# A four-layer decoder on one core: the LSTM's gates turned in two pieces, the third batch's attention moved beside the second batch's picks, and gathers tied to the blocks beside them

## The chip, the cores and the metric

The kernel runs on one core of one Trainium2 chip. The metric is the device time of one execution in microseconds (us); lower is better. The core has a matrix engine (PE), a vector engine (DVE), an activation engine (ACT), a general engine (POOL) and a queue engine (SP), each with an instruction stream of its own that it works off in order. They meet only at semaphores. SP and POOL issue the DMA transfers; POOL alone issues those whose rows are looked up in an index (gathers and scatters).

## The reference, cut to what matters

A batch of 4 sequences of 512 tokens of 256 numbers, `x`, goes through four layers. Each adds a gated attention and then a gated feed-forward block to `x`:

```
x = x + tanh(g_xattn[0]) * L0_xattn(ctx, layernorm(x))   # LSTM that attends to 64 context rows
x = x + tanh(g_ffn[0])   * L0_ffn(layernorm(x))          # 8 experts, the best one
x = x + tanh(g_xattn[1]) * L1_xattn(layernorm(x), ctx)   # attention both ways
x = x + tanh(g_ffn[1])   * L1_ffn(layernorm(x))          # 8 experts, the best two
x = x + tanh(g_xattn[2]) * L2_xattn(layernorm(x), ctx)   # additive attention
x = x + tanh(g_ffn[2])   * L2_ffn(layernorm(x))          # 8 experts, as many as make up 0.8
x = x + tanh(g_xattn[3]) * L3_xattn(layernorm(x), ctx)   # 16 heads
x = x + tanh(g_ffn[3])   * L3_ffn(layernorm(x))          # 8-bit product
```

The three pieces that the change touches:

```
# L0_xattn, one of 512 steps in order
e = tanh(f_proj + (h0 @ Wh)[:, None, :]); alpha = softmax(e . v); attn = alpha @ feats
i, f, g, o = split(x @ W_ih.T + h @ W_hh.T + b)          # four gates of 256
c = sigmoid(f) * c + sigmoid(i) * tanh(g); h = sigmoid(o) * tanh(c)

# L2_xattn: for each token, 64 context rows, 256 features
rho = sum_d w_d * tanh(txt_proj + feat_proj + b); att = softmax(rho); ...

# L2_ffn: probs sorted, kept while their running sum stays under 0.8 (the first always)
y = sum over kept experts of prob * (relu(x @ W1[e] + b1[e]) @ W2[e] + b2[e])
```

## The kernel before, in words

**The LSTM** (`recurrence`, `lstm_step`) takes the first 3444 us. One step turns the state of step t into that of t + 1: PE multiplies `h` (into `psa` and `psf`), DVE turns `psa` into `hw` and adds it to the context's projection (`e`), ACT takes the tanh, PE sums it over the features (`psr`), DVE and ACT make the softmax (`stat`, `al`, `alb`), PE adds the attention's part to the gates in `psf` [128, 256], and then comes the piece that is changed: DVE turns `psf` into `gt` in 32 x 32 blocks (line 958), PE starts the next step's input part in `psf` (`gates_of_x`, line 557), ACT takes one tanh of all four gates (line 961, 32 numbers in each partition), DVE makes `u` and the new cell state from i, f and g (965, 969), ACT its tanh `tcn` (971), DVE the new `h` from gate o and `tcn` (976). The order of these instructions is written out by hand (`pin`). The first layer's experts fill the gaps: a planner (`Later`) hands PE, ACT, DVE, POOL and SP a few of their instructions at fixed places of a step.

**The other three layers** are the tail, 3444 to 5437 us. Here the order is written as generators that yield after each small piece. `weave(main, side, ratio)` emits `ratio` pieces of `side` after each piece of `main`; `chain` and `turns` put generators one after the other and in turns. PE's order is the order of emission (`Ordered`); DVE, ACT, POOL and SP are ordered by the framework's scheduler from priorities and readiness, and each then works in order. A branch closes a basic block, and the scheduler orders within one.

The main lines are the blocks of experts. Tokens of two batches form a group. `picks_of` (by `sorted_by`) ranks the experts of a batch's tokens and scatters each token's row to its experts' places in DRAM (`rows`, line 1306: 8 scatters of 128 rows for each batch in layer 1, 24 in layer 2). `Blocks` then runs over 128 (layer 1) or 256 rows (layer 2) of one expert: `load` fetches rows and weights (SP), `turn` transposes the rows (PE into PSUM, DVE to `xT`, line 1437), `work_1` and `work_2` multiply, `out` copies 128 result rows out of PSUM (`y`) and stores them to `res`. 20 blocks of a group are always emitted (`sure`); `rest` runs any further ones under a branch. A block of layer 2 is 7 pieces (four of the up product, a turn, two of the down product). `b0`, `b1` are layer 1's two groups, `c0`, `c1` layer 2's. `back` gathers the results for each token from `res` (line 1560: 16 gathers for each group in layer 1, 48 in layer 2) into six buffers `yg`, and DVE adds them to `xtok` (line 1552).

The sides are the attentions of the next layer: `additive` (`l2(b)`, 77 pieces; its core is 128 tanh on ACT and their products on PE into `psr`), `heads` and `quantised` for layer 3, and the picks. In the order before, the side of `b1` is: gathers of group 0, attention of batch 0, attention of batch 1 in turns with the picks of batch 0, picks of batch 1. The side of `c0` is the same for batches 2 and 3. The side of `c1` begins with the 48 gathers of layer 2's group 0.

The pieces of the order that the change touches:

Of the kernel before, what the change touches and what calls it, by code (L numbers as in the profile page):

```python
# [24 lines left out]
AF = mybir.ActivationFunctionType  # L25
# [5 lines left out]
NB, S, D = 4, 512, 256  # L31
# [521 lines left out]
def gates_of_x(net, out, ge, t):  # L553

    sel = net.ident.rearrange("p (b t) -> p b t", b=NB)[:, :, t % 32]
    for q in range(4):
        net.tc.keep_in_program_order(net.nc.tensor.matmul(  # L557
            out[32 * q : 32 * q + NB, :], lhsT=sel, rhs=ge[t // 32][:, ts(q, 256)],
            start=True, stop=False,
        ))  # L560
# [330 lines left out]
def lstm_step(net, sp, ps, w, later, ge, t, h, hnew, cnew, ga, ganext):  # L891
    nc = net.nc
    pin = net.tc.keep_in_program_order
    psf = ps["f"]
# [60 lines left out]
    later.fill("PE", SLOT_C)  # L955

    gt = sp.tile([P, 8, 32], FP, name="gt")
    pin(nc.vector.transpose(gt.rearrange("p g b -> p (g b)"), psf))  # L958
    if t + 1 < S:
        gates_of_x(net, psf, ge, t + 1)  # L960
    pin(nc.scalar.activation(  # L961
        ga[:, 0:4].rearrange("p g c b -> p (g c) b"), gt[:, :, 0:NB], AF.Tanh, scale=0.5
    ))
    u = sp.tile([P, 2, 2, NB], FP, name="u")
    pin(nc.vector.scalar_tensor_tensor(
        u.rearrange("p g c b -> p g (c b)"), ga[:, 0:2].rearrange("p g c b -> p g (c b)"), 1.0,
# [22 lines left out]
def weave(main, side, ratio):  # L989

    due = 0.0
    for _ in main:
        due += ratio
        while due >= 1:
            due -= 1
            next(side, None)
    for _ in side:
        pass


def run(pieces):
    for _ in pieces:
        pass


def chain(*gens):
    for g in gens:
        yield from g
# [84 lines left out]
def load_router(net, layer, pool):  # L1093
    nc, a = net.nc, net.a
    m = {"wr": pool.tile([P, KD, NE], FP, name=f"wr{layer}")}
    nc.sync.dma_start(m["wr"], a[f"L{layer}_wr"])
    if layer == 2:
        for n, shape in (("br", [P, NE]), ("b2", [NE, D])):
            m[n] = pool.tile(shape, FP, name=f"m2_{n}")
            src = a[f"L2_{n}"]  # L1100
            nc.sync.dma_start(m[n], src.partition_broadcast(P) if n == "br" else src)
    return m
# [249 lines left out]
class Blocks:  # L1352
# [87 lines left out]
    def out(self, i, half, ps):  # L1440
        y = self.pool.tile([P, D], FP, name=f"y_{self.kind.layer}", bufs=3)
        if i >= self.on_scalar:
            self.t.nc.scalar.copy(y, ps)
        else:
            self.t.nc.vector.tensor_copy(y, ps)
        self.dma(self.got["res"][ds(self.row(i) + half * P, P), :], y)

    def some(self, lo, hi, at=None):
# [95 lines left out]
def back(t, pool, kind, batches, group, got):  # L1544


    net, nc = t.net, t.nc
    due = deque()

    def add():  # L1550
        for y, xj, c in due.popleft():
            nc.vector.scalar_tensor_tensor(xj, y, c, xj, ALU.mult, ALU.add)  # L1552

    for b in batches:
        for i in range(TPB):
            for k in range(0, kind.most, 2):
                here = []
                for kk in (k, k + 1):
                    y = pool.tile([P, D], FP, name="yg", bufs=6)
                    nc.gpsimd.indirect_dma_start(  # L1560
                        out=y[:, :], out_offset=None, in_=got["res"][:, :],
                        in_offset=bass.IndirectOffsetOnAxis(
                            ap=got["index"][:, b - group[0], kk, i : i + 1], axis=0
                        ),
                    )
                    c = got["cw"][:, b - group[0], kk, i : i + 1]
                    here.append((y, net.xtok[:, b * TPB + i, :], c))
                due.append(here)
                if len(due) > 2:
                    add()  # L1570
                yield
    while due:
        add()
        yield
# [23 lines left out]
def gate_bias(t, w, pool):  # L1598

    w["hbg"] = pool.tile([P, 2], FP, name="hbg")  # L1600
    t.nc.vector.tensor_scalar_mul(w["hbg"], w["b"][:, 6, :], 0.5)
# [412 lines left out]
def turns(*gens):  # L2014

    gens = list(gens)
    while gens:
        for g in list(gens):
            try:
                next(g)  # L2020
            except StopIteration:
                gens.remove(g)
            yield


def part_of(gen, n):

    for _ in range(n):
        if next(gen, gen) is gen:
            return  # L2030
        yield
# [3 lines left out]
def gated_blocks_kernel(ctx: ExitStack, tc: tile.TileContext, a, out):  # L2035
    net = Net(ctx, tc, a)
# [18 lines left out]
    }  # L2055
    lstm(net)
    t = Tail(net, ctx)
    t.last = None, None
    mp = ctx.enter_context(tc.tile_pool(name="routers", bufs=1))
    t.rows = mp.tile([P, 3, GB, D], FP, name="rows_in")  # L2060
    t.b1 = mp.tile([P, 3, F_MOE[2] // P], FP, name="b1_in")
    with right, ExitStack() as work:

        def beside(name, bufs):
            return right.enter_context(tc.tile_pool(name=name, bufs=bufs, side="right"))

        p2 = beside("attn2", 1)
        sort, first = beside("sort", 1), beside("first", 2)
        pool = {"sort": sort, "got": mp}
        m = {1: load_router(net, 1, mp), 2: load_router(net, 2, mp)}  # L2070
        with tc.tile_pool(name="attn1", bufs=1) as p1:
            w1 = load_l1(net, p1)
            w2 = load_l2(net, p2)
            gate_bias(t, w1, p1)
            pk = Picks(t, sort)

            def l1(b):
                return both_ways(t, w1, p1, b)

            def l2(b):  # L2080
                return additive(t, w2, p2w, b)

            def behind(layer, part, b):

                return chain(
                    part(b), turns(sorted_by(layer, b), part(b + 1)), sorted_by(layer, b + 1)
                )

            def sorted_by(layer, b):
                g, n = divmod(b, GB)  # L2090
                return picks_of(t, pk, pool, KINDS[layer], m[layer], b, n, got[layer][g])

            b1 = Blocks(t, KINDS[1], first, got[1][1], KINDS[1].sure % 3)
            b0 = Blocks(t, KINDS[1], first, got[1][0], 0, b1)
            run(behind(1, l1, 0))
            weave(b0.sure(), chain(behind(1, l1, 2), constants_l2(t, w2, p2)), 1.1)
            b0.rest()
        one = ctx.enter_context(tc.tile_pool(name="second", bufs=2))
        p2w = work.enter_context(tc.tile_pool(name="attn2_work", bufs=1))
        c1 = Blocks(t, KINDS[2], one, got[2][1], (2 * KINDS[1].sure + KINDS[2].sure) % 3, on_scalar=0)  # L2100
        c0 = b1.next = Blocks(t, KINDS[2], one, got[2][0], 2 * KINDS[1].sure % 3, c1, on_scalar=12)

        def back_of(layer, g, batches=None):
            return back(t, one, KINDS[layer], batches or groups[g], groups[g], got[layer][g])

        weave(b1.sure(), chain(back_of(1, 0), behind(2, l2, 0)), 2.7)
        b1.rest()
        weave(c0.sure(), chain(back_of(1, 1), behind(2, l2, 2)), 2.0)
        c0.rest()
    p3 = ctx.enter_context(tc.tile_pool(name="attn3", bufs=1))  # L2110
    w3 = load_l3(net, p3)
# [125 lines left out]
```

## Time and profile before

Three timed runs took 5443.04, 5443.75 and 5444.30 us (median 5443.75). The profiled execution took 5438.9 us, of which its span from the first instruction to the last is 5437.2.

| | |
|---|---|
| LSTM, 54 to 3444 us | 512 steps, 6.62 us each |
| tail, 3444 to 5437 us | 1993 us |
| busy PE, DVE, ACT, POOL of the span | 4618.9, 2444.1, 2531.7, 467.7 us |
| granted PE clock, mean | 0.959 |
| blocks `b1` with attention of batches 0 and 1 | from 3944 us |
| first row of POOL's 24 scatters of batch 1, layer 2 | 4266.82 us |
| first up product of `c0` | 4309 us |
| first piece of `c1` | 4761 us |
| layer 3 alone | from 5145 us |

A line of the timeline gives start, duration, engine, source line, operation, `out<-in`, shapes and count; in brackets stands how long the engine idled before it and what ended that. A line of the stage windows gives the busy time (and number of records) of PE, PE's weight loads, DVE, ACT and, where it worked, POOL, the granted PE clock as a share of full speed, and DMA. A product in 32-bit numbers leaves two PE records.

### The profile page before, as it was taken

How to read it: one execution, taken by the hardware profiler on the slowest of the kernel's cores; microseconds unless marked ns; L12 is line 12 of the kernel's file. 1: busy time of each engine (PE TensorE's matmuls, PEld its weight loads, DVE VectorE, ACT ScalarE, POOL GpSimd, SP SyncE). 2: the span in 40 equal slices, each digit the busy share in tenths (PEclk: the TensorE clock that was granted, in tenths of full speed). 3: DMA queues.
4: the chain of work that ended last, by engine and by line, in shares of the span. 5: the costliest groups of instructions: out<-in, count | busy, mean ns of one | idle time of the engine just before them, and what ended most of it. 6: DMA issues, size and time to landing. Idle time of an engine off the chain costs nothing. (4 is left out here: it accounts for less than half of the span.)

```text
span 5437.2 us, 139292 instructions
## 1 busy us (share of the span) xinstructions
PE 4618.9 (85%) x57536; PEld 2505.2 (46%) x57536; DVE 2444.1 (45%) x9788; ACT 2531.7 (47%) x7114; POOL 467.7 (9%) x884
## 2 busy tenths in 40 slices
PE   6756698889999899999999989987988599879967
PEld 3222244334444344444444434764533365767734
DVE  4555555555555555555555555224422332222245
ACT  2233465456656566565566556421276166223212
POOL 1000000100100100000000000001111201130030
PEclk9999999999999999999999999988998699889978
DMA  5000012122222122122122211313543333454210
GB/s 196 18 2 2 10 72 109 42 79 97 87 76 95 54 91 95 62 76 95 72 81 79 87 43 56 107 52 126 198 143 128 131 117 129 166 178 142 84 53 8
DMA packets 117964, 480.48 MB, mean 88 GB/s; under 512 B 23473, under 2 KB 62786, under 8 KB 87938
## 3 DMA queue, kind: packets, MB, share of 16 engines
q1 hardware_dynamic: 105026, 437.85, 22.5%
q0 software_dynamic: 12288, 33.57, 1.8%
q8 instruction: 456, 7.47, 0.6%
q14 instruction: 194, 1.59, 0.1%
HBM read 434.65 MB, written 137.89 MB: 105 GB/s over the span
## 5 line engine op out<-in xcount | busy, mean ns | idle before, releaser
L950 PE MATMUL psf<-fw,alb 128*4 128x256 f32 x8192 | 538.7, 380 | 142.4 <-DVE alb L946 111.1
L803 PE MATMUL ps_up<-xm,ring 128*128 128x256 f32 x2048 | 614.8, 412 | 3.4 <-ACT h L813 3.3
L834 PE MATMUL ps_down<-ring,h 128*128 128x256 f32 x2048 | 581.0, 400 | 0.0
L908 PE MATMUL psf<-whh,hb 128*4 128x256 f32 x8176 | 538.0, 381 | 0.0
L803 PEld LDWEIGHTS ps_up<-xm,ring 128*128 128x128 f32 x2048 | 335.9, 188 | 226.7 <-issue 174.1
L938 ACT ACTIVATE al<-psr,stat 128x64 f32<-128x64 f32 x1024 | 313.2, 310 | 272.0 <-DVE stat L937 271.4
L917 ACT ACTIVATE e<-e 128x256 f32<-128x256 f32 x512 | 213.5, 417 | 465.1 <-DVE e L916 464.1
L834 PEld LDWEIGHTS ps_down<-ring,h 128*128 128x128 f32 x2048 | 357.1, 189 | 157.4 <-issue 112.2
L937 DVE TENSOR_REDUCE stat<-psr 128x1 f32<-128x64 f32 x1024 | 229.5, 225 | 417.3 <-PE psr L926 407.7
L916 DVE TENSOR_TENSOR e<-fproj,hw 128x256 f32<-128x256 f32 x1024 | 395.4, 427 | 17.6
L899 PE MATMUL psa<-wh,hb 128*4 128x64 f32 x8176 | 208.3, 219 | 229.4 <-DVE hb L976 228.3
L926 PE MATMUL psr<-e,vrep 128*32 128x64 f32 x16384 | 347.2, 223 | 38.5 <-ACT e L917 33.0
L977 POOL COPY cb<-ga 128x8 f32<-128x8 f32 x512 | 97.9, 191 | 3214.0 <-DVE ga L969 3214.0
L1778 ACT ACTIVATE h<-featT,cx_txtT 128x512 f32<-128x512 f32 x512 | 324.0, 710 | 99.4 <-PE psr L1019 61.2
L557 PE MATMUL psf<-ge,ident 128*4 128x256 f32 x4096 | 318.0, 382 | 60.3 <-DVE gt L958 60.2
L926 PEld LDWEIGHTS psr<-e,vrep 128*32 128x32 f32 x16384 | 260.1, 109 | 223.8 <-ACT e L917 216.4
L958 DVE STREAM_TRANSPOSE gt<-psf 128x256 f32<-128x256 f32 x512 | 230.5, 450 | 292.6 <-PE psf L950 292.2
L961 ACT ACTIVATE ga<-gt 128x32 f32<-128x32 f32 x512 | 116.9, 228 | 525.3 <-DVE gt L958 525.1
L1019 PE MATMUL ps_up<-xT,ring 128*128 128x256 f32 x1280 | 313.2, 396 | 53.6 <-ACT h L1508 26.8
L950 PEld LDWEIGHTS psf<-fw,alb 128*4 128x4 f32 x8192 | 117.1, 84 | 495.0 <-DVE alb L946 493.8
L899 PEld LDWEIGHTS psa<-wh,hb 128*4 128x4 f32 x8176 | 113.7, 85 | 486.8 <-DVE hb L976 486.8
L1019 PEld LDWEIGHTS ps_up<-xT,ring 128*128 128x128 f32 x1280 | 245.8, 197 | 132.9 <-issue 48.2
(410 smaller groups left out, 6595.2 us busy)
## 6 DMA issues: line engine op xcount, KB each, us to landing
ring<-in_L_w_dram SPq DMA_DIRECT2D x208, 1024.0 KB
ring<-in_L_w_dram SPq DMA_DIRECT2D x120, 512.0 KB
res<-y SPq DMA_DIRECT2D x120, 128.0 KB
rows_in<-rows SPq DMA_DIRECT2D x40, 256.0 KB
rows_in<-rows SPq DMA_DIRECT2D x40, 128.0 KB
rows<-in_x_dram SPq DMA_DIRECT2D x2, 1920.0 KB
res<-in_x_dram SPq DMA_DIRECT2D x2, 1920.0 KB
xtok<-in_x_dram SPq DMA_DIRECT2D x4, 512.0 KB
```

The costliest lines, as they stand in the source:

```text
L557: net.tc.keep_in_program_order(net.nc.tensor.matmul(out[32 * q : 32 * q + NB, :], lhsT=sel, rhs=ge[t // 32][:, ts(q, 256)], start=True, st ...
L803: yield nc.tensor.matmul(cell["ps"][:, f % 2, :], lhsT=ex["w"][:, k, ts(f, P)], rhs=box["x"][:, k, :], start=k == 0, stop=k == KD - 1,)
L834: yield nc.tensor.matmul(cell["ps"], lhsT=ex["h"][:, f, ts(p, P)], rhs=ex["down"][:, f, :], start=f == 0, stop=f == 7,)
L899: pin(nc.tensor.matmul(ps["a"][32 * q : 32 * q + NB, :], lhsT=h[:, c, :], rhs=w["wh"][:, c, ts(q, 64)], start=c == 0, stop=c == 1,))
L908: pin(nc.tensor.matmul(psf[32 * q : 32 * q + NB, :], lhsT=h[:, c, :], rhs=w["whh"][:, c, ts(q, 256)], start=False, stop=False,))
L916: pin(nc.vector.tensor_add(e[:, p], w["fproj"][:, p], bc(hw[:, :, ts(p, 2)], 3, SC)))
L926: pin(nc.tensor.matmul(ps["r"][p][ts(2 * b + i, 32), :], lhsT=w["vrep"][:, c, :], rhs=ev[:, ::-1, :] if i else ev, start=c == 0, stop=c == ...
L938: pin(nc.scalar.activation(al[:, p], ps["r"][p], AF.Exp, bias=stat[:, p, 0:1], accum_out=stat[:, p, 1:2]))
L950: pin(nc.tensor.matmul(psf[32 * q : 32 * q + NB, :], lhsT=alb[:, p], rhs=w["fw"][:, p, ts(q, 256)], start=False, stop=p == 1,))
L958: pin(nc.vector.transpose(gt.rearrange("p g b -> p (g b)"), psf))
L1019: return lambda *a, **k: self.tc.keep_in_program_order(fn(*a, **k))
L1778: nc.scalar.activation(h, featT[:, ec, :], AF.Tanh, bias=w["txtT"][:, ec, col : col + 1])
```

## The change

1. `lstm_step`: the turn of `psf` and the tanh are made in two pieces, columns 0 to 192 (gates i, f, g) and 192 to 256 (gate o): turn, tanh, turn, tanh. `gates_of_x` is emitted after both.
2. `out` keeps the instruction that copies a block's result and its basic block in `t.mark`. In `back`, a gather of layer 2 (`kind.most > 2`) gets a semaphore wait on the latest such copy that has been emitted in the same basic block.
3. The picks of batch 1 leave the side of `b1` (ratio 2.3 for 2.7). They run after `b1` and before `c0`, in turns with the first 42 pieces of batch 2's chain (its 8 gathers and their adds, then its attention). The rest of that chain, batch 3's gathers, its attention in turns with the picks of batch 2, and the picks of batch 3 are the side of `c0` (ratio 1.6 for 2.0).

```diff
@@ lstm_step
-    pin(nc.vector.transpose(gt.rearrange("p g b -> p (g b)"), psf))
+    for lo, hi in ((0, 6), (6, 8)):
+        pin(nc.vector.transpose(
+            gt[:, lo:hi].rearrange("p g b -> p (g b)"), psf[:, 32 * lo : 32 * hi]
+        ))
+        pin(nc.scalar.activation(
+            ga.rearrange("p g c b -> p (g c) b")[:, lo:hi], gt[:, lo:hi, 0:NB], AF.Tanh, scale=0.5
+        ))
     if t + 1 < S:
         gates_of_x(net, psf, ge, t + 1)
-    pin(nc.scalar.activation(
-        ga[:, 0:4].rearrange("p g c b -> p (g c) b"), gt[:, :, 0:NB], AF.Tanh, scale=0.5
-    ))
@@ Blocks.out
-            self.t.nc.scalar.copy(y, ps)
+            x = self.t.nc.scalar.copy(y, ps)
...
-            self.t.nc.vector.tensor_copy(y, ps)
+            x = self.t.nc.vector.tensor_copy(y, ps)
+        self.t.mark = x.ins, self.t.net.nc.cur_bb
@@ back
-                    nc.gpsimd.indirect_dma_start(
+                    x = nc.gpsimd.indirect_dma_start(
...
+                    if kind.most > 2 and t.mark[1] is net.nc.cur_bb:
+                        net.tc.add_manual_dep(
+                            x.ins, t.mark[0].name, mybir.DependencyInfo(
+                                mybir.DependencyClass.Sync, mybir.DependencyReason.DATA
+                            ), reason="in step with the blocks beside it",
+                        )
@@ gated_blocks_kernel
-        weave(b1.sure(), chain(back_of(1, 0), behind(2, l2, 0)), 2.7)
+        weave(b1.sure(), chain(back_of(1, 0), l2(0), turns(sorted_by(2, 0), l2(1))), 2.3)
         b1.rest()
-        weave(c0.sure(), chain(back_of(1, 1), behind(2, l2, 2)), 2.0)
+
+        ahead = chain(back_of(1, 1, [2]), l2(2))
+        run(turns(sorted_by(2, 1), part_of(ahead, 42)))
+        weave(
+            c0.sure(), chain(
+                ahead, back_of(1, 1, [3]), turns(sorted_by(2, 2), l2(3)), sorted_by(2, 3)
+            ), 1.6,
+        )
         c0.rest()
```

`part_of(gen, n)` yields the first n pieces of a generator and leaves the rest in it; `behind(layer, part, b)` is `chain(part(b), turns(sorted_by(layer, b), part(b + 1)), sorted_by(layer, b + 1))`.

More of the change, by code (lines that the diff above doesn't have):

```diff
@@ L2057, in gated_blocks_kernel @@
     t = Tail(net, ctx)
-    t.last = None, None
+    t.last = t.mark = None, None
     mp = ctx.enter_context(tc.tile_pool(name="routers", bufs=1))
```

## The prediction

> **What bounds the kernel now.** I read the stage windows first, then the timeline of one LSTM step and the list of who waits for `gt`, then the timeline around the two changed places of the tail. The windows (columns: PE, PE's weight loads, DVE, ACT, POOL, PE clock, DMA):
>
> ```profile
> 54.00:3444.00 3390.00, 2922.02 (x49827) 1379.42 (x49824) 1791.69 (x7971) 1822.99 (x5838) 191.01 (x593) 1.00 0.18 66
> ...
> 3966.00:4222.00 256.00, 227.08 (x943) 88.80 (x941) 73.15 (x216) 189.63 (x314) 23.96 (x25) 0.94 0.37 126
> 4222.00:4271.00 49.00, 35.21 (x117) 23.81 (x116) 26.52 (x116) 9.97 (x15) 3.27 (x4) 0.69 0.12 40
> 4271.00:4309.00 38.00, 1.24 (x5) 0.87 (x5) 4.09 (x11) 0.00 (x0) 28.91 (x30) 0.52 0.55 195
> 4309.00:4328.00 19.00, 10.80 (x38) 8.51 (x38) 10.18 (x29) 0.30 (x1) 6.70 (x7) 0.68 0.49 159
> 4328.00:4776.00 448.00, 414.43 (x2024) 286.37 (x2023) 124.86 (x394) 216.25 (x374) 56.57 (x58) 0.94 0.42 145
> 4776.00:4831.00 55.00, 18.28 (x64) 14.85 (x65) 22.63 (x55) 6.06 (x13) 35.72 (x37) 0.66 0.46 145
> 4831.00:5145.00 314.00, 308.86 (x1513) 248.34 (x1514) 55.09 (x108) 95.03 (x212) 2.08 (x2) 1.00 0.39 135
> ```
>
> In the LSTM no engine is full: a chain through all of them sets each step. In the tail PE is the bound (448 and 314 us at 93% and 98%) but for two holes: from 4271 to 4328 us, while POOL scatters the picks of batch 1, and from 4776 to 4831, while POOL gathers. The chain of a step:
>
> ```profile
> 2001.71 0.45 DVE L958 STREAM_TRANSPOSE gt<-psf 128x256 f32<-128x256 f32 x1 [0.35 <-PE psf L950]
> 2002.26 0.23 ACT L961 ACTIVATE ga<-gt 128x32 f32<-128x32 f32 x1 [1.97 <-DVE gt L958]
> 2002.52 0.18 DVE L965 SCALAR_TENSOR_TENSOR u<-ga 128x16 f32<-128x16 f32 x1 [0.36 <-ACT ga L961]
> ...
> 2002.81 0.17 DVE L969 SCALAR_TENSOR_TENSOR ga<-u 128x8 f32<-128x8 f32 x1
> ...
> 2003.07 0.21 ACT L971 ACTIVATE tcn<-ga 128x8 f32<-128x8 f32 x1 [0.58 <-DVE ga L969]
> ...
> 2003.54 0.41 PE L899 MATMUL psa<-wh,hb 128*4 128x64 f32 x16 [0.28 <-DVE hb L976]
> ```
>
> Each starts when the one above ends. Of the 512 steps, ACT waited for `gt` in these, says the list for that tile; in the other 217 it was still at work on the first layer's gelu:
>
> ```profile
>   DVE gt L958: 525.1, 295
> ```
>
> The second hole, at the start of `c1`:
>
> ```profile
> 4776.12 0.37 ACT L1443 COPY y<-ps_down 128x256 f32<-128x256 f32 x1 [6.74 <-PE ps_down L1019]
> ...
> 4783.26 0.68 DVE L1437 COPY xT<-ps_side 128x512 f32<-128x512 f32 x1
> ...
> 4784.00 7.53 PE L1019 MATMUL ps_up<-xT,ring 128*128 128x256 f32 x24 [8.15 <-DVE xtok L1552]
> ...
> 4811.25 0.37 ACT L1443 COPY y<-ps_down 128x256 f32<-128x256 f32 x1 [34.76 <-remote]
> ...
> 4817.86 3.78 PE L1019 MATMUL ps_up<-xT,ring 128*128 128x256 f32 x8 [26.33 <-ACT h L1508]
> ```
>
> PE stands still twice: 8.15 us because the copy to `xT` lies behind 13 adds of gathered rows in DVE's order, and 26.33 us because ACT can't make its second `y` copy while 36 gathers run back to back at 1.25 us each (4764.66 to 4808.7). It goes on 2.5 us after they stop.
>
> **Change 1, gate o last.** The 64-column turn of `psa` (line 904) takes 251 ns and the 256-column one of `psf` 450: 1.04 ns a column. The first turn, of 192, then takes 383, 67 less. A tanh of 32 takes 228 ns and one of 8 (`tcn`) 208, so one of 24 about 221, 7 less. In 295 steps 74 ns leave the chain, 21.8 us; in the 217 where ACT is late only the 7, 1.5 us. Added: a turn of 64 (251 ns) and a tanh of 8 (208 ns) a step. The turn starts some 70 ns before the first ends (the distance of DVE's neighbours in this step) and ends at 0.56 us after the first began; `u` can't start before 0.73 (turn 0.38, 0.10 to ACT, 0.22, 0.03 back). The tanh runs from 0.70 to 0.91, and `tcn` is due at 1.28. PE's `gates_of_x` starts 0.11 us later, lasts 0.62, and PE next waits for `h` at 1.75. All three are covered by 0.17 us or more; no DMA is moved. In the built program `u` waits for the count of the first tanh alone. Sum: **-23 us**. Bounds: a turn whose cost is proportional to its columns saves 112 ns, -37; a third of the gain lost to the added instructions, -15. Below nothing: the first rival.
>
> The Trainium skill speaks against this part (VectorE: DVE Perf Modes, "The TRN2 errata"): a fixed cost is paid per instruction, so that many small operations pay it many times. The row agrees, 208 ns for a quarter of what takes 228. By that rule with both pieces on the chain the step would lose instead of gain; by the rows above the second piece lies beside `u` and the cell state.
>
> **Change 2, held gathers.** In the built program the 48 gathers of `c1` stand in POOL's order as before, and 8 wait for nothing new; then, following the copies of blocks 0 to 4 (two each), go 2, 8, 2, 4, none, 4, 2, 8, 2, 8, each of the first in such a run with the wait. Behind a waiting gather on POOL are only gathers and one reduction for layer 3's last product; DVE's adds wait for them, and in DVE's order `xT` of block 1 now lies behind 8 adds (13 before), of block 2 behind 10 more (at least 27 before). The stretch 4776 to 4831 has 64 PE records; at the pace of the window after it (314/1513 = 0.2075 us) they take 13.3, so 41.7 us are lost there. What stays: the wait for block 1's `xT`, since the 8th add ended at 4779.7 and PE had been idle since 4775.9, 4 us; and three runs of 10 gathers (blocks 0, 3, 4), each 12.5 us long beside an up product of 7 us and the start of a down product. No row shows such a run alone. Bounds: nothing, as beside block 0, whose 68 records from 4761.36 took 14.5 us against 14.1 at pace; or all of it, 3 x 12.5. I take 4 us each, nearer the first, because a run ends before the next block's second `y` copy is due. So 16 stay: **-26 us**, bounds -38 (41.7 less 4) and 0. The gathers of group 1 (5175 us on) are emitted behind the branch, where no copy is in their basic block, and stay free.
>
> **Change 3, the order around batch 1's picks.** Before, 178 side pieces (all but the 15 of those picks) stand beside 178/2.7 = 66 of `b1`'s 82; now beside 178/2.3 = 77. So 2.75 blocks move into 3966 to 4222. A block there costs PE 7.2 us (from the groups of 3900 to 5300: `ps_up` from `ring` 100.3 us in 193 records, so 8 take 4.2; `ps_down` 53.9 in 216, so 8 take 2.0; its turns some 1) and ACT 1.2; PE has 29 us idle in that window and ACT, which binds (128 tanh at 633 ns a batch), gets 3 us more: +4. Then 1.25 blocks and the pipe's end, 9 us, and the branch (3940.1 to the first gather at 3946.3 between `b0` and `b1`), 6. Batch 1's picks start at 4241 instead of 4224. They took 43 us to the first scatter (4266.8) among blocks; now without blocks, but POOL's order puts all 16 gathers of layer 1's group 1 (20 us) ahead of the scatters and DVE's puts their adds among the picks: I take 40, to 4281. The 24 scatters took 30.3 us (to 4297.1), to 4311. From there to the first up product were 11.7 us, six of them for adds that now come earlier: 8, to 4319, 10 later than 4309. SP's queue: the weights of `c0` still stand behind its rows there, and two down parts that were fetched in the scatters' shadow no longer are: +3. Gained: the halting start 4309 to 4328, whose 38 records are worth 8 of 19 us, -11; and PE work of 36 attention pieces (42 less 6 of the gathers) that moves into the hole: 60 tanh, 120 records at 13.85/104 = 0.133 us (`psr` in a full PE window, 4360 to 4400) = 16, with the products and turns before them 20. Behind 4328 PE is the bound, so these count. Sum 10 + 3 - 11 - 20 = **-18 us**. Bounds: picks in 25 us and a second start at once, -38; tanh at half speed beside the scatters, as in 4120 to 4160 where ACT was busy 19.6 of 40 us, so that 54 tanh (34 us) take 68 from 4281 and c0 starts at 4357, +20.
>
> **Sum**: -23 - 26 - 18 = -67 on the profiled 5438.9, so 5372; the median of the timed runs lies 4.9 above it, so 5443.75 - 67 = **5377 us**.
>
> **The rivals.** (a) *Slower: the second piece of the gates lands on the chain.* If `u` or `tcn` waits until the second tanh is done, that is at 0.91 instead of 0.70, a step gains 0.21 - 0.07 = 0.14 us, over 512 steps +70; with -44 from the rest +26, 5470. It decides once the second piece costs over 0.17 us of cover plus 0.09 (44 us / 512). Against it: the wait of `u` and the margins above. 4%. (b) *The hold only deals the stall out.* Each run of gathers stops PE for its whole length: change 2 gives 0, 5403. For it: 34.76 us of ACT's wait ended with the gathers, so that any run may do it. Against: 8 gathers beside block 0 cost 0.4 us. 13%. The Trainium skill (DMA: Bandwidth & Descriptors, "SWDGE vs HWDGE vs iDMA") says that a DMA engine goes round its queues in turn, so that gathers slow other transfers but don't stop them. SP issued nothing between 4781 and 4811, so this trace can't show it; by that rule the stall would be DVE's order alone, which the new order mends as well. (c) *The start of `c0` slips*, by the tanh at half speed: change 3 costs 20, 5415. 14%. (d) *The change does not do what it says*: 8 of 48 gathers are free anyway, and the scheduler already pulls batch 3's gathers in front of the scatters; with (b) and (c) both, 5441. 5%.
>
> **How the numbers follow.** A difference under 0.2% (11 us) can't be told from none here. My forecast, all three parts within their bounds: 60%, between 5350 and 5400. Better than that (upper bounds of two parts): 4%. (b) 13%, (c) 14%, (d) 5% and (a) 4%. Faster by over 0.2%: 60 + 4 + 13 + 14 = 91, less 3 for the poor ends of (b) and (c), 88; within: 7; slower: 5, which is (a) and a little of (d). The range leaves out (a), (d) and the ends where two parts are extreme: 5338 (-37 -38 -31) to 5424 (-15, 0, -5).
>
> **What would show it.** After, turns of about 383 and 251 ns and tanh of 221 and 208 a step, and a step that is 0.045 us shorter on average (LSTM 3367 us). ACT without a wait of 30 us at the start of `c1`, and PE's idle time in its first five blocks under 20 us. First up product of `c0` near 4319 less the LSTM's 23, its end 18 us nearer to the LSTM's end than before. Wrong if `u` waits for the second tanh, if PE stands still after each `y` copy of `c1`, or if `c0` starts over 30 us later than 4309 in the tail's own time.

## The result, and the profile after

The changed kernel takes 5354.6 us (median; 5351.8 to 5356.0), the kernel before 5443.4: a ratio of 0.9841, with a 95% interval of 0.9824 to 0.9858. That is 89 us less, where 67 were forecast; the time lies in the forecast range of 5338 to 5424. The profiled execution took 5354.89 us, 84.0 less than that of before. These 84 us can be split by events that both traces have:

| stretch of the program | before, us | after, us | difference | forecast |
|---|---|---|---|---|
| to the last `hb` of the LSTM | 3444.3 | 3421.1 | -23.2 | -23 |
| from there to the first up product of `c0` | 864.5 | 879.8 | +15.3 | +10, and +3 for weights |
| from there to the first up product of `c1` | 452.6 | 411.0 | -41.6 | -31 |
| from `c1`'s first up product to the second group's gathers | 415.4 | 383.0 | -32.4 | -26 |
| the rest | 260.4 | 258.2 | -2.2 | 0 |

The windows of the changed kernel, with the same columns as those of before (PE, weight loads, DVE, ACT, POOL, the granted clock, the DMA engines' share, GB/s), laid around the same stages:

```profile
54.00:3421.00 3367.00, 2927.77 (x49824) 1380.53 (x49825) 1823.03 (x8483) 1874.42 (x6350) 190.01 (x593) 1.00 0.18 67
3943.00:4208.00 265.00, 237.02 (x1016) 99.76 (x1014) 79.28 (x226) 191.12 (x317) 23.99 (x25) 0.94 0.39 127
4208.00:4258.00 50.00, 25.53 (x83) 13.38 (x82) 30.29 (x124) 18.40 (x28) 15.71 (x16) 0.62 0.16 48
4258.00:4289.00 31.00, 23.91 (x70) 4.71 (x68) 1.94 (x15) 20.85 (x34) 23.27 (x24) 0.94 0.27 98
4289.00:4310.00 21.00, 18.71 (x81) 7.39 (x81) 3.32 (x7) 18.21 (x30) 0.00 (x0) 0.84 0.91 350
4310.00:4722.00 412.00, 383.62 (x1849) 279.40 (x1848) 121.82 (x390) 165.54 (x296) 54.42 (x56) 0.94 0.43 151
4722.00:4805.00 83.00, 76.75 (x355) 65.95 (x354) 29.10 (x65) 21.98 (x53) 39.50 (x41) 0.98 0.68 232
```

Both holes are filled. Beside the scatters of batch 1's picks (4258 to 4289, 24 instructions on POOL) PE is busy for 24 us of 31, where it had 1.2 of 38; in the stretch of `c1`'s gathers (4722 to 4805) it is busy for 77 of 83, where it had 18 of 55. What got longer is the stretch ahead of the scatters, 4208 to 4258, in which DVE has the picks and the adds of gathered rows together.

One step of the LSTM after, the same chain as was shown of before (`x2` in the row of `gt` or `ga` are the two pieces):

```profile
2037.88 0.51 DVE L959 STREAM_TRANSPOSE gt<-psf 128x192 f32<-128x192 f32 x2 [0.74 <-PE psf L950]
2038.36 0.34 ACT L962 ACTIVATE ga<-gt 128x24 f32<-128x24 f32 x2 [1.90 <-DVE gt L959]
2038.61 0.18 DVE L968 SCALAR_TENSOR_TENSOR u<-ga 128x16 f32<-128x16 f32 x1 [0.22 <-ACT ga L962]
2038.90 0.17 DVE L972 SCALAR_TENSOR_TENSOR ga<-u 128x8 f32<-128x8 f32 x1
2039.16 0.21 ACT L974 ACTIVATE tcn<-ga 128x8 f32<-128x8 f32 x1 [0.47 <-DVE ga L972]
...
2039.62 0.41 PE L899 MATMUL psa<-wh,hb 128*4 128x64 f32 x16 [0.20 <-DVE hb L979]
```

From the turn to the next step's first product it is 1.74 us, before 1.83. `u` starts 0.25 us after the first tanh does, while both pieces of the tanh together end 0.34 after it: `u` doesn't wait for the second. Over all steps the median falls from 6532 to 6459 ns in those where ACT waits for the turn, and from 6659 to 6649 in those where ACT is late.

The start of `c1` after, PE alone, four of its blocks:

```profile
4728.78 7.17 PE L1022 MATMUL ps_up<-xT,ring 128*128 128x256 f32 x32 [0.67 <-DVE xT L1440]
...
4745.53 8.86 PE L1022 MATMUL ps_up<-xT,ring 128*128 128x256 f32 x32 [2.23 <-DVE xT L1440]
...
4775.83 7.07 PE L1022 MATMUL ps_up<-xT,ring 128*128 128x256 f32 x32
...
4792.48 7.17 PE L1022 MATMUL ps_up<-xT,ring 128*128 128x256 f32 x32 [2.24 <-DVE xT L1440]
```

All 32 records of a block's up product come in one run of 7 to 9 us. The waits of 8.15 and 26.33 us have become waits of 0.7 to 2.2 us for `xT`.

### The profile page after: what moved, and what is told of

It is laid out like the page before. It is cut to its first block, busy times and chain, and to the rows that moved or that the text cites. A ratio compares the mean times of both kernels' runs of the same rounds, so it can differ in the third digit from the quotient of the medians.

```text
span 5353.2 us, 140684 instructions
## 1 busy us (share of the span) xinstructions
PE 4626.1 (86%) x57536; PEld 2505.0 (47%) x57536; DVE 2474.6 (46%) x10300; ACT 2581.3 (48%) x7626; POOL 466.2 (9%) x884
## 5 line engine op out<-in xcount | busy, mean ns | idle before, releaser
L834 PE MATMUL ps_down<-ring,h 128*128 128x256 f32 x2048 | 581.8, 400 | 0.0
L962 ACT ACTIVATE ga<-gt 128x24 f32<-128x24 f32 (+1 forms) x1024 | 169.2, 214 | 508.3 <-DVE gt L959 507.6
L959 DVE STREAM_TRANSPOSE gt<-psf 128x192 f32<-128x192 f32 (+1 forms) x1024 | 263.0, 295 | 294.3 <-PE psf L950 294.0
L1022 PE MATMUL ps_down<-ring,h 128*128 128x256 f32 x1280 | 294.7, 387 | 3.5 <-issue 2.4
```

What stands on the lines that cost most here:

```text
L834: yield nc.tensor.matmul(cell["ps"], lhsT=ex["h"][:, f, ts(p, P)], rhs=ex["down"][:, f, :], start=f == 0, stop=f == 7,)
L959: pin(nc.vector.transpose(gt[:, lo:hi].rearrange("p g b -> p (g b)"), psf[:, 32 * lo : 32 * hi]))
L1022: return lambda *a, **k: self.tc.keep_in_program_order(fn(*a, **k))
```

## The experiments

Each kernel was timed against the kernel before on the same chip. The first four ran on one chip (before: 5443.3 us), the next four on another (5437.4), the last four on two more, where the kernel before took 5354.4 and 5354.0 us. Where kernels of different chips are compared, the difference of their ratios, times 5443, is given.

### The three parts, each alone

`gate_alone` has only this hunk on top of the kernel before:

```diff
-    pin(nc.vector.transpose(gt.rearrange("p g b -> p (g b)"), psf))
+    for lo, hi in ((0, 6), (6, 8)):
+        pin(nc.vector.transpose(
+            gt[:, lo:hi].rearrange("p g b -> p (g b)"), psf[:, 32 * lo : 32 * hi]
+        ))
+        pin(nc.scalar.activation(
+            ga.rearrange("p g c b -> p (g c) b")[:, lo:hi], gt[:, lo:hi, 0:NB], AF.Tanh, scale=0.5
+        ))
```

> The kernel before with change 1 alone: the turn and the tanh of the gates in two pieces, gate o last. My theory: the LSTM of the changed kernel ended 23.2 us earlier than before (3421.1 against 3444.3), and nothing after it depends on the gates, so this kernel gives those 23 us and no more: 5443.75 - 23 = 5421, between 5417 and 5425. Rival: part of the LSTM's gain comes from the other two changes (pieces of the tail's code that move within it): then less than 15 us here. A second rival: the tail loses something with this change alone; then the time before the last hb is 23 us shorter, and the whole is not.

Measured: 5412.1 us (5409.0 to 5424.6), ratio 0.9941 (0.9924 to 0.9957), which is 31 us less, with 23 to 41 in the interval. The median lies outside of 5417 to 5425, but the kernel's own runs are 15 us apart, and the trace has the forecast steps: medians of 6458 and 6649 ns, the changed kernel's to 1 ns. In its trace the LSTM ends at 3424.8 us, 19.4 sooner than before. Over all traces the LSTM with the old step ends between 3442.0 and 3448.2 us and with the new one between 3416.3 and 3424.8, so the 23 us of the LSTM are this part's, give or take some 4. The trace doesn't show a further 8; its profiled run was the slowest of the four, at 5424.6.

`hold_alone` has only the held gathers:

```diff
+        self.t.mark = x.ins, self.t.net.nc.cur_bb
...
+                    if kind.most > 2 and t.mark[1] is net.nc.cur_bb:
+                        net.tc.add_manual_dep(
+                            x.ins, t.mark[0].name, mybir.DependencyInfo(
+                                mybir.DependencyClass.Sync, mybir.DependencyReason.DATA
+                            ), reason="in step with the blocks beside it",
+                        )
```

> The kernel before with change 2 alone: the 48 gathers at the start of c1 held to the copies of y. In the changed kernel the part from c1's first up product to the second group's gathers took 383.0 us, before 415.4. My theory: these 32 us are the hold's: 5443.75 - 32 = 5412, between 5407 and 5420. Rival: c1 of the changed kernel is also quicker because it starts in another state (change 3 leaves other work to c0's end); then a gain of 20 us or less, and PE's idle time over 4 us at the start of c1 doesn't vanish.

Measured: 5412.4 us (5410.5 to 5414.2), ratio 0.9942 (0.9926 to 0.9959): 31 us less. That is what the `c1` stretch gained in the changed kernel (32.4); in this kernel's own trace the stretch is 27.6 us shorter than before (387.8 for 415.4). So little of the gain, if any, is owed to change 3.

`order_alone` has only the new order:

```diff
-        weave(b1.sure(), chain(back_of(1, 0), behind(2, l2, 0)), 2.7)
+        weave(b1.sure(), chain(back_of(1, 0), l2(0), turns(sorted_by(2, 0), l2(1))), 2.3)
         b1.rest()
-        weave(c0.sure(), chain(back_of(1, 1), behind(2, l2, 2)), 2.0)
+        ahead = chain(back_of(1, 1, [2]), l2(2))
+        run(turns(sorted_by(2, 1), part_of(ahead, 42)))
+        weave(
+            c0.sure(), chain(
+                ahead, back_of(1, 1, [3]), turns(sorted_by(2, 2), l2(3)), sorted_by(2, 3)
+            ), 1.6,
+        )
```

> The kernel before with change 3 alone: the third batch's attention begun beside the second one's picks, with the new ratios. From the end of the LSTM to c1's first up product the changed kernel took 1290.8 us, before 1317.1. My theory: these 26 us are this part's, and c1 keeps its stall of some 34 us: 5443.75 - 27 = 5417, between 5411 and 5424. Rival: the stall at the start of c1 is already weaker here, since other work lies beside it: 5395 or less. Second rival: c0 can't keep the gain without the hold: 5430 or more.

Measured: 5417.0 us (5415.9 to 5418.4), ratio 0.9951 (0.9935 to 0.9968): 26 us less, and the stall of `c1` is there as before (ACT waits 32 us ahead of a copy to `y`). The three parts alone make 31 + 31 + 26 = 88 us, all together 89. Each of these numbers is uncertain by some 9 us, so within that the parts add up, and none is seen to take from another.

### Is it the wait, the order, or the burst?

`hold_without_wait` keeps the tie between a gather and a copy to `y` for the order of issue, and drops the wait:

```diff
-                                mybir.DependencyClass.Sync, mybir.DependencyReason.DATA
+                                mybir.DependencyClass.NoSync, mybir.DependencyReason.DATA
```

> Change 2 with its order and without its wait: the gathers are tied to the copies of y for the order in which instructions are issued alone, so DVE has the adds between the copies to xT as in the held kernel (8 ahead of block 1's, 10 ahead of block 2's), but POOL waits for nothing new. Theory one, the burst: 34.76 us of ACT's wait ended with the burst of gathers, and no order of DVE changes that: the stall of 26 us stays, only the first one of 8 shrinks: 5443.75 - 4, between 5432 and 5445, with an ACT wait over 20 us ahead of a copy to y. Theory two, DVE's order (and the Trainium skill, DMA: Bandwidth & Descriptors, SWDGE vs HWDGE vs iDMA, by which gathers slow other transfers and don't stop them): the stall goes as with the hold: 5412, between 5405 and 5420.

Measured: 5418.9 us (5415.9 to 5422.7), ratio 0.9958 (0.9941 to 0.9974): some 24 of the 31 us come without any wait. The two intervals overlap; in the traces the `c1` stretch took 394.2 us here, 387.8 in `hold_alone` and 415.4 before, so 21 of 28. The time is that of theory two, but the trace shows another way to it. From the timeline of this kernel:

```profile
4794.33 0.94 POOL L1561 DMA_INDIRECT yg<-res,g_index  x1 [0.30 <-issue]
4805.66 1.07 POOL L1561 DMA_INDIRECT yg<-res,g_index  x1 [10.39 <-DVE xtok L1553]
```

```profile
4791.77 0.38 PE L1019 MATMUL ps_up<-xT,ring 128*128 128x256 f32 x1 [2.49 <-issue]
4800.01 3.78 PE L1019 MATMUL ps_up<-xT,ring 128*128 128x256 f32 x8 [7.87 <-ACT h L1509]
```

```profile
4798.85 0.37 ACT L1443 COPY y<-ps_down 128x256 f32<-128x256 f32 x1 [21.72 <-remote]
```

The gathers still start as a burst, and ACT and PE still fall behind in it. But it ends after 24 gathers, not 36: the 25th has to wait for a buffer `yg` that an add on DVE sets free, and in the new order that add lies behind the copy to `xT` of a block that PE hasn't reached. So with the new order the six buffers hold the gathers, after a stall; the wait holds them ahead of it. All 48 gathers took 91 us here, 90 in the held kernel, 69 before.

`burst_beside_blocks` prices the burst by itself: 40 gathers that nobody reads, in one run, in the middle of `c1`.

```diff
+    def burst(n):
+        for j in range(n):
+            y = one.tile([P, D], FP, name="yg", bufs=6)
+            x = nc.gpsimd.indirect_dma_start(
+                out=y[:, :], out_offset=None, in_=got[2][0]["res"][:, :],
...
+            )
+            if not j:
+                net.tc.add_manual_dep(
+                    x.ins, t.mark[0].name, mybir.DependencyInfo(
...
+        yield
...
-        back_of(2, 0, [0]), turns(constants_l3(t, w3, p3), back_of(2, 0, [1])), layer3(0), layer3(1)
+        back_of(2, 0, [0]), turns(constants_l3(t, w3, p3), back_of(2, 0, [1])), burst(40),
+        layer3(0), layer3(1)
...
-    weave(c1.sure(), part_of(start, 93), 0.7)
+    weave(c1.sure(), part_of(start, 94), 0.7)
```

> The changed kernel with 40 gathers more (rows of layer 2's results that nobody reads), issued in one run from a block in the middle of c1 on, where no other gather is about; the first is held to a copy of y, nothing waits for their end. It prices a burst by itself, without adds on DVE. Theory one, the burst stops the engines: with the gate part alone, PE made one product of ps_up each 2.8 us while 35 gathers ran back to back; 40 gathers take 50 us, and after the first dozen PE falls to such a pace: 15 to 35 us more, 5370 to 5390. Theory two, DVE's order alone: the burst costs what its transfers take from the weights' ones, under 4 us: 5352 to 5359 (and by the Trainium skill, DMA: Bandwidth & Descriptors, SWDGE vs HWDGE vs iDMA, a queue more slows the others' transfers and doesn't stop them).

Measured: 5390.8 us (5385.3 to 5397.3), ratio 0.9913 (0.9895 to 0.9931), against 0.9841 of the changed kernel: 39 us more. The windows of this kernel over the first 13 gathers, over the rest of the burst, and behind it:

```profile
4801.00:4818.00 17.00, 16.14 (x79) 14.07 (x78) 0.69 (x1) 3.70 (x9) 12.29 (x13) 1.00 0.70 240
4818.00:4855.00 37.00, 9.53 (x22) 4.64 (x20) 0.00 (x0) 0.37 (x1) 25.54 (x27) 0.55 0.36 103
4855.00:4870.00 15.00, 12.26 (x37) 7.96 (x37) 1.39 (x2) 5.16 (x12) 0.00 (x0) 0.75 0.48 167
```

And PE and ACT in it, from the timeline:

```profile
4841.66 0.59 PE L1022 MATMUL ps_up<-xT,ring 128*128 128x256 f32 x1 [1.52 <-issue]
4844.46 0.59 PE L1022 MATMUL ps_up<-xT,ring 128*128 128x256 f32 x1 [2.21 <-issue]
4847.26 0.59 PE L1022 MATMUL ps_up<-xT,ring 128*128 128x256 f32 x1 [2.21 <-issue]
```

```profile
4819.99 0.37 ACT L1446 COPY y<-ps_down 128x256 f32<-128x256 f32 x1 [11.32 <-remote]
4855.72 0.37 ACT L1446 COPY y<-ps_down 128x256 f32<-128x256 f32 x1 [35.35 <-remote]
```

For 13 gathers PE is at its pace. Then it leaves one record of a product mostly each 2.1 to 2.8 us for as long as the burst lasts, waiting for nothing that the profile shows, and ACT waits 35 us for a product that PE finished long before. The times of the semaphores' updates, which the trace keeps too, show what ACT waits for: PE's last record for the second copy ends at 4815.14 us, but PE's semaphore, on which the copy waits, moves at 4855.65, 0.07 us before the copy begins. The store that had to free the copy's buffer had landed by 4800.17. In the kernel before it was the same: the product of the second copy ends at 4775.85, and PE's semaphore moves at 4811.18. Some updates beside a burst are missing from the record, but these two are the ones that let the copies begin. So it is the signal between the engines that comes 35 to 41 us late, not the product and not a store behind the gathers.

DVE has nothing to do in the 37 us, so no order of DVE can be the cause. The burst by itself stops the other engines, and theory one holds. Nor are the DMA engines full: they are busy for 0.36 of the time. The rule of the Trainium skill that the rival leaned on (DMA: Bandwidth & Descriptors, "SWDGE vs HWDGE vs iDMA", queues served in turn) speaks of transfers; what stands still here is the engines, in a stretch in which the gathers were nearly all that the DMA engines had to move (27 of 128 KB each, 3.5 of 3.8 MB), so the rule gives no bound for it.

### What fills the hole beside the picks

`few_ahead` leaves in front of `c0` only the gathers of batch 3's first half of work:

```diff
-        run(turns(sorted_by(2, 1), part_of(ahead, 42)))
+        run(turns(sorted_by(2, 1), part_of(ahead, 6)))
```

> The changed kernel with 6 pieces of batch 3 beside batch 2's picks in place of 42: the gathers and their adds alone, none of the attention. My theory: PE loses the work that it did in the hole (24 of 31 us busy beside the scatters, 19 of the 21 after them), and c0 gets it back; the picks come some us sooner without the turns and products between: 20 to 28 us more, 5375 to 5383, with PE idle for 25 us or more beside the scatters. Rival: the scheduler pulls the pieces ahead anyway, since in the written order only the gathers' place is fixed: 5352 to 5360. Second rival: the gain of change 3 came from the gathers and the ratios and not from the pieces: 5352 to 5362, with c0 as short as in the changed kernel.

Measured: 5374.5 us (5366.6 to 5381.8), ratio 0.9883 (0.9863 to 0.9902): 23 us more than the changed kernel, as in my theory. PE beside the scatters and after them:

```profile
4246.00:4277.00 31.00, 0.00 (x0) 0.00 (x0) 1.82 (x14) 0.00 (x0) 23.29 (x24) 0.50 0.27 98
4277.00:4298.00 21.00, 13.65 (x49) 10.09 (x50) 5.19 (x10) 5.26 (x8) 0.00 (x0) 0.70 0.90 344
```

The scatters begin 7 us sooner, counted from the LSTM's end, and `c0` 10 us sooner; but `c0` then takes 437 us to `c1`'s first up product (4723.1 less 4286.3), 26 more than in the changed kernel, and `c1` 7 more. So the attention in the hole is worth 26 us in `c0` and costs 10 ahead of it. The rest of `c0`'s gain, 16 of the 42 us, comes without it: from the gathers and adds that now lie ahead of `c0`, or the ratios, which this run doesn't tell apart.

`gathers_behind_picks` takes batch 3's gathers out of the first half of the picks:

```diff
-    nc.scalar.copy(combT, ps.rearrange("p i t -> p (i t)"))
+    x = nc.scalar.copy(combT, ps.rearrange("p i t -> p (i t)"))
+    t.mark = x.ins, nc.cur_bb
...
-                    if kind.most > 2 and t.mark[1] is net.nc.cur_bb:
+                    if (kind.most > 2 or b == 2) and t.mark[1] is net.nc.cur_bb:
...
+        picks = sorted_by(2, 1)
+        for _ in picks:
+            if t.mark[1] is net.nc.cur_bb:
+                break
-        run(turns(sorted_by(2, 1), part_of(ahead, 42)))
+        run(turns(picks, part_of(ahead, 42)))
```

> The changed kernel with the third batch's 8 gathers held to the copy to combT of batch 2's picks, so that their adds leave the first half of the picks, where DVE needs 50 us from the end of batch 2's attention to the first scatter (before 40). Theory one: the adds are what made the picks 10 us longer; the scatters begin 8 us sooner, and the attention of batch 3 some us later: 5346 to 5352. Theory two: POOL has the 16 gathers ahead of the scatters, so that holding the gathers holds the scatters: no gain or up to 8 us lost, 5354 to 5363.

Measured: 5361.1 us (5358.3 to 5366.0), ratio 0.9860 (0.9844 to 0.9877): 10 us more by the ratios, which overlap with the changed kernel's. The scatters do begin 6 us sooner (831 us after the LSTM's end, not 837), and theory one is right so far. But the tanh of batch 3 begin later, PE has their products in front of the first block's in its order, and `c0` begins 885 us after the LSTM, not 880. What the picks gain, the attention behind them loses.

### The second piece on the chain

`two_turns_one_tanh` puts both pieces of the turn on the chain, which is what the slower rival feared, in its mildest form:

```diff
-    pin(nc.vector.transpose(gt.rearrange("p g b -> p (g b)"), psf))
+    for lo, hi in ((0, 6), (6, 8)):
+        pin(nc.vector.transpose(
+            gt[:, lo:hi].rearrange("p g b -> p (g b)"), psf[:, 32 * lo : 32 * hi]
+        ))
+    pin(nc.scalar.activation(
+        ga.rearrange("p g c b -> p (g c) b")[:, 0:8], gt[:, :, 0:NB], AF.Tanh, scale=0.5
+    ))
```

> The kernel before with the turn in two pieces, and one tanh of 32 that waits for both: the second piece stands on the chain, as in the rival on gate o. Theory from the rows of the changed kernel: there the second turn ended 130 ns after the first (449 after 319, from the first hb of a step), that is 513 ns after the first began, where the one turn of before took 450. So 63 ns more in the 292 steps in which the tanh waits for the turn, and nothing in the 219 in which ACT is late by more (it began 171 ns after the turn's end, and needs about 95): 292 x 0.063 = +18, 5443 + 18 = 5461, between 5455 and 5467. Rival, a fixed cost of each instruction in full: 383 + 251 = 634 ns, 184 more in 292 steps and about 108 in 219: +77, 5520. Third: the chain does not run through the turn: within 4 us of before.

Measured: 5459.8 us (5457.8 to 5464.4), ratio 1.0041 (1.0026 to 1.0055): 22 us slower, and the LSTM ends at 3464.4 us, 20 after that of before. The rows of the turn's tile, with the times that ACT waited for it:

```profile
L959 DVE STREAM_TRANSPOSE gt<-psf x1024: 205/291/385, 52.0 to 3462.9; 128x192 f32<-128x192 f32 x171
...
  DVE gt L959: 545.9, 296
```

The second turn costs the chain some 63 ns, not the 184 of a row of its own length: it runs mostly beside the first. So the gain of change 1 rests on `u` needing no word of the second piece; with one wait more the same two pieces lose what they now win.

### Spaces between the transfers

Runs of 24 scatters stop PE as the gathers do. The windows of the changed kernel over two of them, beside `b1` (the first 18 us and the rest) and beside `c0` (the last third):

```profile
4103.00:4121.00 18.00, 13.52 (x62) 4.77 (x54) 2.21 (x12) 10.01 (x17) 13.73 (x15) 1.00 0.50 170
4121.00:4136.00 15.00, 5.43 (x16) 2.17 (x16) 1.38 (x2) 2.61 (x5) 9.43 (x10) 0.75 0.49 166
...
4450.00:4465.00 15.00, 8.11 (x10) 0.87 (x9) 0.00 (x0) 2.89 (x4) 9.52 (x10) 0.59 0.27 98
```

PE is busy for 5.4 and 8.1 of 15 us in the last parts. Beside `b1` it is busy for only 13.5 of 18 us over the first 15 scatters, so the number that does no harm is not the same everywhere. Four kernels put small clears of a spare tile (128x224) on POOL between the transfers:

```diff
+def spaced(net, x, last, clears=2):
...
+    no = mybir.DependencyInfo(mybir.DependencyClass.NoSync, mybir.DependencyReason.DATA)
+    if last is not None:
+        net.tc.add_manual_dep(x.ins, last.ins.name, no, reason="apart")
+    m = x
+    for _ in range(clears):
+        m = net.nc.gpsimd.memset(net.spare_tile, 0.0)
+        net.tc.add_manual_dep(m.ins, x.ins.name, no, reason="apart")
+        x = m
+    return m
```

`burst_spaced` puts them into the burst of 40 gathers:

> The kernel with 40 gathers beside the blocks of c1, as before, but POOL clears a small spare tile twice after each gather (128x224; one of 128x128 takes 205 ns, so 0.27 us each by its size): one gather in about 1.85 us in place of 1.25. The burst alone cost 36 us, and PE kept its pace for the first 13 gathers. Theory one, a backlog: gathers come faster than something behind them is worked off, and engines stand still when it is full; with the spaces it never fills: PE at pace, 5354 to 5360, with the run of gathers taking 75 us. Theory two, a number: any run of more than a dozen starves the others, however spaced: 5385 to 5420. Theory three, a share: each gather costs PE 0.9 us wherever it stands: 5390 as without the spaces.

`spaced_scatters` puts them into the scatters of batches 0, 2 and 3:

> The changed kernel with the same two small clears on POOL after each of the 24 scatters of layer 2's picks of batches 0, 2 and 3 (not of batch 1, for whose rows c0 waits). In the changed kernel PE is busy 5.4 of 15 us, 8.1 of 15 and 5.3 of 16 in the last third of these three runs (from 4121, 4450 and 4621 us), and at over 90% ahead of them and behind. By the backlog theory these 27 us go, less what PE has to wait for anyway: 20 to 27 us less, 5328 to 5335. By the theory of a number the runs of 24, now 45 us long each, starve PE for longer: 5365 to 5400. If PE's work there is hidden behind something else: 5350 to 5358.

`spaced` has these and the second group's gathers:

> The same, and the 48 gathers of layer 2's second group spaced as well (from 5095 us, 67 us long, where PE is busy 32 of 68 us at a granted clock of 0.63, beside layer 3). Theory: in that stage the waits are those of one batch's chain through PE, DVE and ACT, stretched by semaphores that come late; spaced gathers take 90 us, but the 24 of batch 2 end 15 us later than now. So between 10 us less than with the scatters alone and 12 us more; if layer 3's chain is what binds and the gathers aren't, it is less.

`spaced_by_dose` has the scatters again, with two clears, one, or one for two scatters:

> The changed kernel with spaces between the scatters of three of layer 2's batches, of three sizes: batch 0 two clears of POOL's spare tile after each scatter, batch 2 one, batch 3 one after every second; batch 1 has none and shows whether runs of 24 starve PE here at all (in the changed kernel they did, and on the chip of the last three kernels they did not). If they do here: by the backlog theory PE keeps over 90% beside batch 0 and batch 2, where it had 36% and 54% in the last third of the run, and batch 3 tells whether an eighth more room is enough; 15 to 27 us less than the changed kernel, 5328 to 5340 where the kernel before takes 5443. By the theory of a number PE falls behind after the 13th scatter in all three: 5355 to 5380. If they don't here, PE is full beside all four, and the time is that of the last but one kernel, 5280 where the kernel before takes 5354: the spaces then cost and gain nothing.

Measured: 5282.1 us (ratio 0.9863, 0.9847 to 0.9879), 5280.5 (0.9865, 0.9849 to 0.9882), 5319.0 (0.9937, 0.9920 to 0.9954) and 5278.7 (0.9858, 0.9842 to 0.9874). They say little of the spaces, for on these chips runs of 24 don't stop PE. The windows of `burst_spaced` over the last parts of the same two runs as above, which have no spaces in it:

```profile
4115.00:4130.00 15.00, 14.95 (x71) 5.27 (x70) 2.35 (x5) 14.63 (x25) 9.80 (x11) 1.00 0.70 226
...
4420.00:4435.00 15.00, 15.00 (x84) 9.81 (x84) 2.77 (x7) 9.94 (x16) 10.20 (x11) 1.00 0.62 200
```

The same instructions, at the same pace on POOL, and PE is full. In `spaced_by_dose`, on the other chip, batch 1's 24 scatters have no spaces, and ACT is busy for 30.7 of the 31 us beside them. The signals are on time as well: in `burst_spaced` each update of PE's semaphore beside these two runs comes within 0.13 us of the end of its record. What the runs do show: 40 spaced gathers in `c1` cost next to nothing here (5282 us with them, 5280 in `spaced_scatters` without), and the second group's spaced gathers cost 38 us (5319 against 5280), more than the 12 that I had allowed. Their run became 38 us longer too (99.7 us for 61.7), and layer 3's last two batches need these rows. Whether spaces help on a chip where bursts stop PE stays open, and so does a version that beats the changed kernel: none of these is shown to.

## Why the prediction was right, point by point

**Change 1 (-23 forecast, -23.2 in the trace).** Right in each step that stands on the chain. The first turn took 383 to 385 ns (383 forecast), the first tanh 222 (221); off the chain the second turn took 207 ns, not 251, and the second tanh ended 0.82 us after the first turn began, not 0.91, so there was more room than forecast; a step in which ACT waits lost 73 ns (74), one in which ACT is late 10 (7). The slower rival's point of decision, `u` waiting for the second piece, did not come about, and the run with one tanh behind both turns shows that its mechanism is real, but that a second turn costs 63 ns there and not its own 251. Of the Trainium skill's rule (VectorE: DVE Perf Modes, "The TRN2 errata", a fixed cost of each instruction), which the page states for operations that read SBUF, the trace bears out the size of small rows of tanh. Two turns in a row, which read PSUM, did not cost the sum of two on the chain.

**Change 2 (-26 forecast, -31 alone, -32.4 in the trace).** The mechanism was right: PE stood still because ACT could not copy during the burst, and that goes when the burst is dealt out. The term that was mis-sized is "three runs of 10 gathers ... 4 us each" and 4 us for the wait on `xT`: of these 16 us, what is left at the start of `c1` is 0.7 + 2.2 + 2.2 + 1.1 us. Runs of up to 10 gathers cost next to nothing here, which fits the burst, whose first 13 do no harm. The rival "the hold only deals the stall out" fell with it. What the prediction did not see is that DVE's new order alone, by way of the six buffers, gives some 24 of the 31 us. And "ACT can't make its second `y` copy" stops one step short: what came late was PE's signal to ACT.

**Change 3 (-18 forecast, -26 alone, -26.3 in the trace).** The late picks came as forecast: the scatters began at 4258.4 us, forecast 4281 less the LSTM's 23; they ended at 4288.7, forecast 4311 less 23; `c0` began at 4300.9, 2 us behind what 4319 and 3 for the weights less 23 give. The tanh at half speed, the rival that put `c0` off, showed only in the last third of the scatters, and did not put it off by more than that. The work moved was right too: 120 records of `psr` lie in the hole, the number that was forecast, and `c0` lost 13 us of them and 6 of the products ahead (forecast 16 and 4). The mis-sized term is the -11 for the halting start: `c0`'s up products became 8 us shorter (157.9 to 150.0 us for as many records), and PE's idle time in `c0` fell by 13 (from 41.7 of 452.6 us to 28.4 of 411.0), together 21. With hardly any attention ahead, `c0` was still 16 us shorter than before, so most of this is not the attention's.

**The sum.** 23 + 26 + 18 = 67 was forecast, and 23.2 + 32.4 + 26.3 + 2.2 = 84.1 came in the profiled execution. Nearly all of the miss lies in two terms that were taken too low: 6 us of waits in `c1` that did not stay, and the start of `c0`, whose 10 us more were partly spent by a start 2 us later. Another 2 us fell behind the second group's gathers, where nothing was forecast; that stretch differs by as much between kernels that do the same there (256.4 us in `hold_alone`, 260.4 before).

## What to carry to other kernels

Do not let a long run of indirect transfers stand beside work that is bound by another engine: in `c1` 13 in a row did no harm, and each further one cost 1.4 us of the whole kernel's time (39 us for 27), on the chips whose runs stop PE. A stall that one engine shows (ACT, 35 us, "remote") may come from a queue that none of its data goes through: ask what ran back to back at that time, and test it with a burst that nobody reads. A split on a serial chain pays when the consumer needs only the first piece; check in the built program what it waits for, since one wait more turns -23 us into +22.

## What was not expected of the hardware

Beside a burst of indirect transfers from POOL, at 1.25 us each, PE and ACT ran at normal pace for the first 13, then nearly stopped until the burst was over: one record of PE mostly each 2.1 to 2.8 us, a wait of ACT of 35 us, with the DMA engines busy for 0.36 of the time. What ACT waited for was PE's signal, 40.5 us behind the end of the product. Runs of 24 scatters do much the same.

It is not so on every chip: on two of the chips runs of 24 left PE full, and the kernel before took 5354 us there, 1.5 to 1.6% less than on the others (5437 and 5443). That the missing stalls are these 85 us was not shown, since the kernel before has no trace from there; nor was the changed kernel timed there. But `burst_spaced` is the changed kernel with 40 spaced gathers more, and its trace can be laid beside the changed kernel's. Of the 73.8 us between them 1.8 fall in the LSTM and 2.2 in `c1`, whose gathers are held; 28.4 fall between the LSTM and `c0`, 24.6 in `c0` and 16.8 behind `c1`, the stretches with unbroken runs of 16, 24 and 48 transfers. So the chips differ where such runs stand. And 72 us of saving are left on a chip where runs of 24 don't stop PE (5354.4 less 5282.1); how much of that is the hold's there isn't known. Why the signals come late, and why only on some chips, is open.
